# First half's projected attention tiles: scale and shift on ScalarE with a shift from Pool

## The chip, the cores and the metric

The kernel runs on one core of a Trainium2 chip. The core has five engines that each work through a queue of their own, in order: TensorE (PE, matrix products; PEld is its loading of weights), VectorE (DVE), ScalarE (ACT), GpSimd (POOL) and SyncE (SP, which here issues DMAs). An instruction that waits for a semaphore holds up all that stands behind it in its queue. The metric is the device time in microseconds (us) of one execution; the median of several runs is taken. TensorE adds up its products in PSUM, eight banks of 128 x 512 fp32 numbers.

## The reference

One transformer block on x of 8 x 1024 x 512 in fp32, causal attention with 16 heads of 32, and a feed-forward part with a sine in it:

```python
x = x + _layernorm(_L0_attn_ref(_layernorm(x), Wqvk, Wo))
x = x + _layernorm(_L0_ffn_ref(_layernorm(x), W1, b1, phases, w_real, w_imag, W2, b2))
# _layernorm: (x - mean) / sqrt(var + 1e-5), over the last axis
# _L0_attn_ref: qvk = h @ Wqvk; scores = q k^T, causal mask, / sqrt(512); softmax; @ v; @ Wo
# _L0_ffn_ref: hidden = x @ W1 + b1; hidden + coef * sin(theta + 0.1 hidden); relu; @ W2 + b2
```

The change lies in the first line, in the outer `_layernorm`: the attention's output, projected by Wo, is normalised row by row and then added to x.

## The kernel before, in words

The batches are worked one after the other (the loop at the end of `tile_block_kernel`, L923). For a batch, `attention` runs over four groups of four heads. In a group, `find_maxima` forms the row maxima of the scores, and then the scores are computed a second time, transposed, in units of keys: three units for the first half of the 512 + 512 queries, seven for the second half (`KEY_UNITS`, L428; the sixth holds key blocks 5 and 7). `weigh` does one unit: a product with minus one subtracts the maximum (L577), a second adds the scores (L588), both into two PSUM tiles of two banks; ScalarE takes the exponential of each PSUM tile into `w` (L603), and for key blocks on the diagonal Pool blanks the upper triangle (L607). `weighted_values` multiplies with v (L626), one unit later than the scores. In the second half the softmax's denominators are formed by adding up the `w` tiles on VectorE (L655), and one product with ones at the end (L641).

`finish_block` projects a half of the queries by Wo and does both layer norms around it, four tiles of 128 rows each, as a generator of stages. Stage by stage, one tile apart, these are: `project` (four products, L771; ScalarE copies the result to `ys`, L780; VectorE forms mean and variance, `moments`, L225 and L226; the reciprocal root), `add` (normalise y, L785 by way of `normalised` at L244, and add to x, L786), moments of the new x, `scale` (normalise x into `xn`, L244) and `transpose` (on TensorE, L111, with a copy by ScalarE, L262, into `x2T`, the feed-forward part's input). In each step of the generator the later stages come first.

For the first half of the queries, half 0, the generator is advanced inside the last head group, once per unit of keys of the second query half, from its second unit on. So this chain on VectorE and ScalarE runs interleaved with the exponentials L603, the selections L607 and the adds L655. Half 1 is worked in the beginning of the feed-forward part. The reciprocal root is formed by ScalarE in half 0, as exp(-0.5 ln(var + eps)) (`rstd_by_scalar`, L239 and L240), and by Pool in half 1 (`rstd_of`, L232 and L233).

The feed-forward part (`feed_forward`) runs over 2 x 16 chunks: products with W1 (L819), Identity with the bias on ScalarE (L827), the reduction of the angle on VectorE, the sine on ScalarE (L834, with its own table load once per batch), the combination on VectorE (L837, L838), and products with W2 (L846).

Two things set the order of the work. `in_order` pins an instruction to its place among the pinned ones of its engine; what is not pinned is placed by the scheduler of the tile framework by its own costs, as are the copies L780, the moments and the roots. And PSUM banks are handed out by `psum` to the tile that is free longest (L81): the second PSUM tile of a unit's scores uses the banks that the first exponential of the unit before it empties. The tiles `yp`, `xn`, `inverse` and `xin` share a pool of five buffers.

Of the kernel before, what the change touches and what calls it, by code (L numbers as in the profile page):

```python
# [11 lines left out]
F32 = mybir.dt.float32  # L12
BF16 = mybir.dt.bfloat16
AF = mybir.ActivationFunctionType
ALU = mybir.AluOpType

P = 128
# [14 lines left out]
def kernel(  # L32
# [14 lines left out]
    nc = tc.nc  # L47
# [22 lines left out]
    small = ctx.enter_context(tc.tile_pool(name="small", bufs=4))  # L70
# [10 lines left out]
    def psum(shape, dtype=F32):  # L81
        size = math.prod(shape[1:]) * (2 if dtype == BF16 else 4)
        n = -(-size // (4 * HALF))
        free = [k for k in range(0, 8, n) if None not in done_at[k : k + n]]

        def rank(k):
            halved = n == 1 and done_at[k ^ 1] is None and done_at[k] + 2 <= clock[0]
            return not halved, max(done_at[k : k + n])

        k = min(free, key=rank)  # L90
        t = banks[:, k : k + n, :].rearrange("p b n -> p (b n)")[:, : size // 4]
        if dtype != F32:
            t = t.bitcast(dtype)
        if len(shape) == 3:
            t = t.rearrange("p (a b) -> p a b", a=shape[1])
        done_at[k : k + n] = [None] * n
        banks_of[id(t)] = list(range(k, k + n)), t
        return t

    def drained(t, n=None):  # L100

        mine = banks_of[id(t)][0]
        for k in [mine[0]] if n is None and len(mine) == 1 else mine if n is None else [mine[n]]:
            clock[0] += 1
            done_at[k] = clock[0]

    def in_order(instruction):
        tc.keep_in_program_order(instruction)
# [56 lines left out]
    for n in range(2):  # L165
        t = const.tile([P, TPB, P], BF16, tag=f"parts_q{n}", name=f"parts_q{n}")
# [55 lines left out]
    def moments(src, mv):  # L222

        st = small.tile([P, 6], F32, tag="st", name="st", bufs=3)
        nc.vector.bn_stats(st, src)  # L225
        nc.vector.bn_aggr(mv, st)  # L226
# [16 lines left out]
    def normalised(dst, src, mv, rs):  # L243
        return nc.vector.tensor_scalar(dst, src, mv[:, 0, 0:1], rs, ALU.subtract, ALU.mult)  # L244

    def one_mv():
        return small.tile([P, 1, 2], F32, tag="mv1", name="mv1", bufs=6)

    def staged(n, *stages):


        for s in range(n + len(stages) - 1):
            for k in reversed(range(len(stages))):
                if 0 <= s - k < n:
                    stages[k](s - k)
            yield True

    def transpose_rows(src, dst, evacuate):
        pt = psum([P, KC, P])
        for kc in range(KC):  # L260
            transpose_on_pe(pt[:, kc, :], src[:, kc * P : (kc + 1) * P], ident)
        evacuate(dst, pt)  # L262
        drained(pt)
# [489 lines left out]
    def finish_block(b, half, wvT, x2T):  # L753


        x2T[half] = tp.tile([P, KC, HALF], F32, tag="t", name=f"x2T_{b}_{half}")
        ys, xns, mvs, rss = {}, {}, {}, {}

        def x(t):
            return xt[b, half * TPB + t]  # L760

        def measure(t, source):
            mvs[t] = one_mv()
            moments(source, mvs[t][:, 0, :])
            rss[t] = (rstd_of if half else rstd_by_scalar)(mvs[t], 1)

        def project(t):
            y = psum([P, D])
            for kc in range(KC):
                in_order(  # L770
                    nc.tensor.matmul(  # L771
                        y,
                        wvT[:, kc, t * P : (t + 1) * P],
                        wo_sb[:, kc, :],
                        start=(kc == 0),
                        stop=(kc == KC - 1),
                    )
                )
            ys[t] = tmp.tile([P, D], F32, tag="tmp", name="yp")
            nc.scalar.copy(ys[t], y)  # L780
            drained(y)
            measure(t, ys[t])

        def add(t):
            in_order(normalised(ys[t], ys[t], mvs[t], rss[t]))  # L785
            in_order(nc.vector.tensor_add(x(t), x(t), ys[t]))  # L786

        def scale(t):
            xns[t] = tmp.tile([P, D], F32, tag="tmp", name="xn")
            normalised(xns[t], x(t), mvs[t], rss[t])  # L790

        def transpose(t):
            transpose_rows(xns[t], x2T[half][:, :, t * P : (t + 1) * P], nc.scalar.copy)

        return staged(TPB, project, add, lambda t: measure(t, x(t)), scale, transpose)


# [125 lines left out]
    for b in range(B):  # L923
        load_tables()
        wvT = [tp.tile([P, KC, HALF], F32, tag="t", name=f"wvT_{b}_{n}") for n in range(2)]
        x2T = {}

        def after(g, b=b, wvT=wvT, x2T=x2T, rest=rest):


            if g == 0:
                return rest, len(KEY_UNITS[0])
            if (b, g) == (0, 1) and B > 1:
                return measure_ahead(1), 2
            if g == NG - 2 and b + 1 < B:
                return norm1(b + 1), 0
            if g == NG - 1:
                return finish_block(b, 0, wvT[0], x2T), len(KEY_UNITS[0]) + 1
            return iter(()), 0

        before = attention(b, wvT, after)
        rest = feed_forward(b, x2T, before, finish_block(b, 1, wvT[1], x2T))
# [44 lines left out]
```

## Time and profile before

| what | value |
|---|---|
| median of 3 runs | 3884.76 us (3884.75 to 3884.77) |
| the profiled execution's own time | 3884.87 us |
| its span in the trace | 3883.2 us |
| TensorE (PE) busy | 98% |
| VectorE (DVE) busy | 71% |
| ScalarE (ACT) busy | 40% |
| Pool busy | 15% |
| TensorE clock granted | 0.996 of full speed |
| DVE normalising `yp` (L244) | 64 instructions, 540 ns each |
| one batch, from one first L771 to the next | 479.0 us (259.27 to 738.31) |

A group's line in the profile has the source line, the engine, the operation, what it writes and reads, the shapes and the count, then the busy time in us and the mean of one in ns, then how long the engine stood idle just before them and what ended that. A line of the waits names who waited for whom, the time in total, the number of times and the longest. A line of a timeline has start and duration in us, the instruction and, in brackets, the idle time before it. The line numbers are those of the kernel before; helpers such as `normalised` (L244), `moments` (L225, L226) and `transpose_on_pe` (L111) serve several callers, so the tile's name tells which.

### The profile page before, as it was taken

What the parts mean: (1) busy time and instruction counts of PE and PEld (TensorE: products, weight loads), DVE (VectorE), ACT (ScalarE), POOL (GpSimd) and SP (SyncE); (2) the same over time, 40 slices, a digit from 0 to 9 for tenths busy, and PEclk for the clock granted to TensorE, in tenths of its full rate; (3) what the DMA queues carried; (4) which work ended last, traced back from release to release, by engine and by line L of the source; (5) the groups of instructions that cost most, each with busy time, mean ns of one, the idle gap of its engine ahead of it and who ended that gap; (6) DMA issues with size and microseconds to landing.
All of it is one profiled execution on the core that took longest, in us unless ns stands there. A gap on an engine that the chain in (4) does not pass through costs nothing. (4 is left out here: it accounts for less than half of the span.)

```text
span 3883.2 us, 51435 instructions
## 1 busy us (share of the span) xinstructions
PE 3800.5 (98%) x19457; PEld 1764.2 (45%) x19457; DVE 2748.0 (71%) x6105; ACT 1542.1 (40%) x2960; POOL 567.7 (15%) x1060
## 2 busy tenths in 40 slices
PE   8999999999999999999999999999999999999998
PEld 4444444444444444444444444444444444454443
DVE  4777767777676777767777677777677776777666
ACT  4552145521465214642156421564215642156311
POOL 1211021110211102111022100211002120021100
PEclk9999999999999999999999999999999999999999
DMA  4000000000000001000010000100001000000000
GB/s 155 26 20 22 22 31 11 16 22 22 31 15 12 22 22 33 12 12 22 22 33 12 12 22 22 34 12 12 22 22 33 12 12 0 22 23 12 1 0 22
DMA packets 43495, 86.42 MB, mean 22 GB/s; under 512 B 4144, under 2 KB 4208, under 8 KB 42736
## 3 DMA queue, kind: packets, MB, share of 16 engines
q1 hardware_dynamic: 39056, 71.61, 5.8%
q10 hardware_dynamic: 4192, 11.53, 0.8%
q8 instruction: 152, 2.49, 0.3%
q14 instruction: 95, 0.78, 0.1%
HBM read 66.36 MB, written 16.78 MB: 21 GB/s over the span
## 5 line engine op out<-in xcount | busy, mean ns | idle before, releaser
L819 PE MATMUL banks<-x2T,w_sb 128*128 128x512 f32 x2048 | 921.6, 593 | 5.8 <-ACT x2T L262 5.8
L846 PE MATMUL banks<-w_sb,hid 128*128 128x512 f32 x1536 | 690.5, 592 | 0.0
L603 ACT ACTIVATE w<-banks 128x1024 f32<-128x1024 f32 (+1 forms) x640 | 565.7, 937 | 241.7 <-PE banks L588 236.9
L819 PEld LDWEIGHTS banks<-x2T,w_sb 128*128 128x128 f32 x2048 | 386.0, 190 | 478.4 <-issue 468.8
L655 DVE TENSOR_TENSOR w<-w 128x1024 f32<-128x1024 f32 (+2 forms) x448 | 443.9, 1028 | 212.1 <-PE banks L626 125.3
L502 DVE CUSTOM_DVE_ANT_0 es<-banks,mask 128x128 f32<-128x128 f32 (+3 forms) x1024 | 433.0, 486 | 125.5 <-PE banks L472 125.5
L834 ACT ACTIVATE u<-u 128x512 f32<-128x512 f32 x256 | 161.1, 629 | 865.3 <-DVE u L196 842.1
L373 PE MATMUL banks<-xnT,wqvk_sb 128*128 128x512 f32 x1024 | 480.9, 609 | 3.0 <-DVE mx L490 3.0
L846 PEld LDWEIGHTS banks<-w_sb,hid 128*128 128x128 f32 x1536 | 291.8, 190 | 367.4 <-issue 328.4
L607 POOL TENSOR_SCALAR_AFFINE_SELECT w<-w 128x256 f32<-128x256 f32 x512 | 285.2, 576 | 881.6 <-ACT w L603 835.3
L490 DVE TENSOR_REDUCE mx<-banks 128x1 f32<-128x512 f32 (+1 forms) x384 | 309.9, 862 | 103.8 <-PE banks L472 103.8
L827 ACT ACTIVATE hid<-banks,prm 128x512 f32<-128x512 f32 x256 | 175.5, 686 | 473.6 <-PE banks L819 473.5
L829 DVE TENSOR_SCALAR u<-hid,prm 128x512 f32<-128x512 f32 x256 | 123.9, 484 | 308.0 <-ACT hid L827 308.0
L626 PE MATMUL banks<-w,v 128*32 128x512 f32 (+3 forms) x3072 | 325.5, 499 | 5.2 <-POOL w L607 4.3
L588 PE MATMUL banks<-qk 32*128 32x512 f32 (+3 forms) x3072 | 327.7, 491 | 0.0
L472 PE MATMUL banks<-qk 32*128 32x512 f32 (+3 forms) x3072 | 315.2, 510 | 0.6 <-DVE mx L502 0.6
L837 DVE SCALAR_TENSOR_TENSOR hid<-u,coef,hid 128x512 f32<-128x512 f32 x256 | 192.0, 750 | 161.7 <-ACT u L834 161.7
L373 PEld LDWEIGHTS banks<-xnT,wqvk_sb 128*128 128x128 f32 x1024 | 182.8, 190 | 243.3 <-issue 186.7
L522 ACT ACTIVATE es<-es,mx 128x512 f32<-128x512 f32 (+3 forms) x512 | 279.6, 551 | 2.0 <-DVE mx L502 2.0
L394 PEld LDWEIGHTS banks<-wqvk_sb,xnT 128*128 128x128 f32 x2048 | 239.0, 192 | 57.9 <-issue 34.4
L394 PE MATMUL banks<-wqvk_sb,xnT 128*128 128x128 f32 x2048 | 259.5, 280 | 0.0
L771 PE MATMUL banks<-wo_sb,wvT 128*128 128x512 f32 x512 | 234.3, 600 | 0.0
(102 smaller groups left out, 3408.3 us busy)
## 6 DMA issues: line engine op xcount, KB each, us to landing
xin<-in_L_attn_h_dram SPq DMA_DIRECT2D x112, 256.0 KB, 2.8
x<-in_L_attn_h_dram SPq DMA_DIRECT2D x64, 256.0 KB, 2.6
out_dram<-x SPq DMA_DIRECT2D x64, 256.0 KB, 2.0
w_tail<-in_L_ffn_W_dram SPq DMA_DIRECT2D x8, 1024.0 KB, 5.3
w_sb<-in_L_ffn_W_dram ACTq DMA_DIRECT2D x1, 4096.0 KB, 15.5
wqvk_sb<-in_L_attn_Wqvk_dram ACTq DMA_DIRECT2D x3, 1024.0 KB, 9.5
w_sb<-in_L_ffn_W_dram ACTq DMA_DIRECT2D x1, 3072.0 KB, 25.3
wo_sb<-in_L_attn_Wo_dram ACTq DMA_DIRECT2D x1, 1024.0 KB, 6.1
```

The source lines that it names most:

```text
L373: nc.tensor.matmul(pq, wqvk_sb[:, kc, c0 : c0 + P], xnT[b, half][:, kc, :], start=(kc == 0), stop=(kc == KC - 1),)
L394: nc.tensor.matmul(pv[:, t - t0, :], xnT[b, t // TPB][:, kc, (t % TPB) * P : (t % TPB + 1) * P], wqvk_sb[:, kc, c0 : c0 + P], start=(kc == 0),
L472: nc.tensor.matmul(scs[j // 2][:, j % 2, at : at + n], t[r, 0, i * P : (i + 1) * P], t[r, 1, k0 : k0 + n], start=True, stop=True,)
L490: nc.vector.tensor_reduce(out=mx[:, m], in_=sc[:, m, cols], op=ALU.min, axis=mybir.AxisListType.X,)
L502: nc.vector.tensor_tensor_reduce(out=es[:, m, cols], in0=sc[:, m, cols], in1=mask[:, HALF - n :], scale=1.0, scalar=FMAX, op0=ALU.add, op1 ...
L588: nc.tensor.matmul(sts[j // 2][:, j % 2, cols], t[r, 1, kb * P : (kb + 1) * P], t[r, 0, q0 : q0 + n], start=False, stop=True,)
L603: in_order(nc.scalar.activation(w[:, :, :width], st[:, :, :width], AF.Exp, scale=-1.0))
L607: select = nc.gpsimd.affine_select(out=square, in_=square, compare_op=ALU.is_ge, fill=0.0, base=0, pattern=[[0, 2], [1, P]], channel_multi ...
L626: nc.tensor.matmul(acc[r, HALF - n :], v[b, g][:, kb, r], weights[j // 2][:, j % 2, cols], start=first and k == 0, stop=last and k == len( ...
L655: in_order(nc.vector.tensor_add(t[:, :, q], t[:, :, q], w[:, :, cols]))
L819: nc.tensor.matmul(ph, w1_sb[:, kc, fc * P : (fc + 1) * P], x2T[half][:, kc, :], start=(kc == 0), stop=(kc == KC - 1),)
L846: nc.tensor.matmul(ys[half, t], hids[c // 2][:, c % 2, t * P : (t + 1) * P], w2_sb[:, fc, :] if fc < NW2 else w2_tail[:, fc - NW2, :], sta ...
```

## The change

For half 0, the four tiles of each batch that are worked inside the last head group, y is no longer normalised by one VectorE instruction with two operations, (y - mean) x rstd. Instead Pool forms a column of shifts, mean x rstd x (-1), behind the moments and the root of each tile, and ScalarE writes y x rstd + shift over y, as an Identity with a scale and a bias per partition. The addition to x stays on VectorE. Both new instructions are pinned to the program order. Half 1 is as before.

```diff
-        ys, xns, mvs, rss = {}, {}, {}, {}
+        ys, xns, mvs, rss, shifts = {}, {}, {}, {}, {}
...
             measure(t, ys[t])
+            if half == 0:
+
+                shifts[t] = small.tile([P, 1], F32, tag="rs1", name="shift", bufs=4)
+                in_order(
+                    nc.gpsimd.tensor_scalar(
+                        shifts[t], mvs[t][:, 0, 0:1], rss[t][:, 0:1], -1.0, ALU.mult, ALU.mult
+                    )
+                )
 
         def add(t):
-            in_order(normalised(ys[t], ys[t], mvs[t], rss[t]))
+            if half == 0:
+                in_order(
+                    nc.scalar.activation(
+                        ys[t], ys[t], AF.Identity, bias=shifts[t], scale=rss[t][:, 0:1]
+                    )
+                )
+            else:
+                in_order(normalised(ys[t], ys[t], mvs[t], rss[t]))
             in_order(nc.vector.tensor_add(x(t), x(t), ys[t]))
```

The shifts take their buffers from the pool `small`, under the tag of the single roots `rs` (four buffers of 128 x 1 that the roots and the shifts now share).

## The prediction

> **What bounds the kernel now.** I read the engine shares first, then the list of waits for TensorE, then the timeline of one batch around the change on each engine, then the groups by form for the prices.
>
> ```profile
> span 3883.2 us, 51435 instructions
> PE 3800.5 (98%) x19457; PEld 1764.2 (45%) x19457; DVE 2748.0 (71%) x6105; ACT 1542.1 (40%) x2960; POOL 567.7 (15%) x1060
> ...
> PE banks L577 <- ACT w L603: 20.1, 34, 1.7
> ```
>
> TensorE (PE) is busy 98% of the span. A change on the other engines is worth only what it does to PE's gaps, and the largest gap that recurs is the wait of L577 for L603: 20.1 us. The timelines of single batches show where it lies: in each of the eight batches one wait of 1.74 or 1.75 us, in the last attention group, which is where the change works. In batch 0 (start, duration, work; the bracket is the idle time before it):
>
> ```profile
> 280.34 0.34 PE L577 MATMUL banks<-mT,minus 32*128 32x384 bf16 x4
> ...
> 285.20 0.39 PE L577 MATMUL banks<-mT,minus 32*128 32x256 bf16 x2 [1.75 <-ACT w L603]
> ```
> ```profile
> 280.44 0.59 ACT L780 COPY yp<-banks 128x512 f32<-128x512 f32 x1 [1.08 <-PE banks L771]
> 283.52 0.48 ACT L239 ACTIVATE rs<-mv,eps 128x1 f32<-128x1 f32 x2 [2.49 <-DVE mv L226]
> 283.91 0.33 ACT L240 ACTIVATE rs<-rs 128x1 f32<-128x1 f32 x2
> 284.15 1.92 ACT L603 ACTIVATE w<-banks 128x1024 f32<-128x1024 f32 x2
> ```
> ```profile
> 277.43 0.55 DVE L244 TENSOR_SCALAR yp<-yp,mv,rs 128x512 f32<-128x512 f32 x1 [0.51 <-ACT rs L240]
> 278.01 0.69 DVE L786 TENSOR_TENSOR x<-x,yp 128x512 f32<-128x512 f32 x1
> 279.01 1.23 DVE L655 TENSOR_TENSOR w<-w 128x1024 f32<-128x1024 f32 x1 [0.30 <-POOL w L607]
> 280.53 1.23 DVE L655 TENSOR_TENSOR w<-w 128x1024 f32<-128x1024 f32 x1 [0.30 <-POOL w L607]
> 281.68 0.54 DVE L244 TENSOR_SCALAR xn<-x,mv,rs 128x512 f32<-128x512 f32 x1
> ```
>
> I call the key units of the second query half U0 to U6, and the four tiles 0 to 3. PE can't write the second half of U6's scores until the first exponential of U5 (L603) has emptied its banks. U5's scores are there at about 281.6, but ScalarE (ACT) reaches that exponential only at 284.15: ahead of it in its queue stands the logarithm of tile 3's variance (L239), which waits 2.49 us for VectorE's (DVE) moments. So the chain is DVE's queue, then ACT's queue, then PE. PE has no slack in it: whatever delays ACT ahead of U5's exponential delays PE, one for one.
>
> **What the change removes.** 4 x 8 = 32 normalisations on DVE, 540 ns each by the group L244 yp: 17.3 us of DVE, of which at most the three ahead of tile 3's moments (3 x 0.54 = 1.6 us a batch) lie on the chain.
>
> **What it adds.** 32 ACT instructions and 32 shifts of 128x1 on Pool. The nearest rows:
>
> ```profile
> L827 ACT ACTIVATE hid<-banks,prm 128x512 f32<-128x512 f32 x256 | 175.5, 686 | 473.6 <-PE banks L819 473.5
> ...
> L662 ACT ACTIVATE inverse<-inverse 128x512 f32<-128x512 f32 x32 | 20.2, 630 | 1.0
> L660 ACT ACTIVATE inverse<-banks 128x512 f32<-128x512 f32 x32 | 19.1, 597 | 72.7 <-PE banks L641 72.7
> ```
> ```profile
> L232 POOL TENSOR_SCALAR rs<-mv x136: 215/226/1962, 4.9 to 3876.9; 128x1 f32<-128x1 f32 x136
> ```
>
> L827 is the same function with one per-partition operand, from PSUM; L660 has none: 686 - 597 = 89 ns for an operand. From SBUF, as here, without one: 630 (L662). With bias and scale both per partition: 630 + 2 x 89 = 0.81 us. [...] Priced by L827 as it stands it would be 0.69, and the sum below 0.12 x 8 = 1 us smaller; I take 0.81. No table load: Identity already runs in this kernel beside Sin without one of its own, and the instruction order of the built program has no more loads than before. A shift costs 0.23 us (median of L232), up to 1.96 at the worst. Roots and shifts now share four buffers, so every fifth one waits for the readers of the first; the tightest, tile 3's shift in the buffer of tile 2's root, comes at 285.2 in the walk below, 5 us after its last reader: no cost. No DMA is added or moved past another; one load of the input (L306) per batch gains a wait for ACT on its buffer, for an instruction that ended long before. PE's order is identical.
>
> **What it moves.** The instruction order on ACT now reads, for tile t: copy, logarithm and exponential for tile t, logarithm for x of tile t-1, first exponential of the scores, exponential for x, Identity, second exponential of the scores. For tile 3 the Identity stands ahead of both exponentials of U5. On DVE the add x + y now waits for ACT, and for tiles 1 and 2 it stands between the two L655 adds. I walk batch 0 from the rows above (hand-over of 0.03 to 0.1 us as the rows show; back-to-back ACT work overlaps by 0.09).
>
> Tile 0: Identity at 266.9, right after U2's exponentials, done 267.7; DVE is in L655 until 268.4. Hidden: the next step on DVE waits for the copy at 269.4 anyway.
>
> Tile 1: logarithm at 270.83 (before 270.90). U3's first exponential ends 272.46. DVE has been empty since 270.94; before, it filled that gap with the normalisation and the add. Now L655, add, L655 and xn start at 272.50; from start to start they take 1.14 + 0.60 + 1.14 + 0.46, so the next moments begin at 275.84, not 275.43: 0.41 late. That is what DVE gives back: 0.55 less work, but it begins 1 us later.
>
> Tile 2: logarithm at 277.23, U4's first exponential 277.86 to 278.86, Identity to 279.68, second exponential to 280.59 (before 279.36). Pool's first selection ends 279.37; DVE L655 to 280.63, add to 281.24. Pool's second selection comes in only behind DVE's two-input work, about 0.26 us after it (as at 279.48 to 280.50 before): 281.5. The second L655 starts 281.53, before 280.53: DVE is now 1.0 us late, and tile 3's moments are ready at 284.51.
>
> Tile 3: logarithm 284.53, exponential to 285.06, logarithm and exponential for x of tile 2 to 285.50; the shift meanwhile, 285.16 to 285.40, while DVE waits; Identity 285.41 to 286.22; U5's first exponential starts at 286.13. Before: 284.15. **Late by 1.98 us**, of which 1.01 is DVE's lag and 0.97 the longer chain on ACT. PE's wait grows from 1.75 to about 3.7 us.
>
> Behind it: Pool's selections of U5, of which five of the eight batches lost 0.24 + 0.41 us before (L626 waits for L607). Now the second exponential comes when DVE is in L655, so one selection can hold PE for up to 0.5 us, while U6's exponentials come early and the 0.65 goes. 8 x 0.5 - 5 x 0.65 = 0.8 us at one end, -3.3 at the other; I take zero. The sums at L641 need the adds, done at about 292.3, and PE comes there at about 293.2: covered by 0.9 us. In the feed-forward part PE has dense work and the chain starts anew.
>
> Sum: 8 x 1.98 = 15.8 us on the profiled execution's 3884.87 us (1.7 us more than its span; the median of the runs is 3884.76): 3900.7, say **3901**. With 0.6 of DVE lag and 0.69 of Identity it is 1.45 a batch, 3896.5; with a shift held up by one DVE instruction (0.54) and the 0.5 for the selection 3.0 a batch, 3909. Own range 3896 to 3910.
>
> **The rivals.**
> Relief of DVE (not slower). If DVE were the queue that counts and always had work, tile 3's moments would come 1.62 us earlier, at 281.9; with the same ACT chain of 1.60 us U5's exponential starts at 283.5, 0.65 earlier than now: 8 x 0.65 = 5.2, 3880. If Identity also hid, the whole 1.75 would go: 8 x 1.75 = 14, 3871. [...] The trace's windows give DVE 27.6 us busy of 45.3 from 255.34 to 300.66, 61%: busy, not saturated, and its stops are for ACT. It decides where U3's and U4's first exponentials come before DVE runs empty: for U3 some 1.5 us earlier than I find (DVE empty at 270.94, exponential done at 272.46). 12%, half of it faster by over 0.2%.
> Only the chain. DVE makes up its lag, and 0.97 a batch remains: 8 x 0.97 = 7.8, 3893. For it: my 0.6 us at the second selection rests on a Pool operation that yields. 10%.
> Pool is starved. L232's longest of 1.96 us and L607's 1.02 beside L655 against 0.41 alone show that Pool waits for DVE:
>
> ```profile
> 278.57 0.41 POOL L607 TENSOR_SCALAR_AFFINE_SELECT w<-w 128x256 f32<-128x256 f32 x1 [25.39 <-ACT w L603]
> 279.48 1.02 POOL L607 TENSOR_SCALAR_AFFINE_SELECT w<-w 128x256 f32<-128x256 f32 x1 [0.51 <-ACT w L603]
> ```
>
> A shift of tile 3 of 1.96 instead of 0.23 adds 1.7 us, tile 2's some 0.2: 3.9 a batch, 8 x 3.9 = 31, 3916. It decides once tile 3's shift ends later than 285.41. Against it: at all four moments DVE stands idle waiting for ACT (264.6, 271.4, 277.8, 285.2). 10%.
>
> **How the numbers follow.** 68% for 3901, 12% for relief, 10% for only the chain, 10% for starvation. A measurement of this kernel tells about 0.2% (7.8 us) from no change. Faster 6%; same 11% (the other half of relief, half of only the chain); slower 83%. The range from 3886 to 3918 leaves out relief and the upper end of starvation, some 15%.
>
> **What would show it.** L577's wait for L603 goes from 20.1 to about 36 us, one wait of about 3.7 us a batch; DVE waits for ACT ahead of L655 in U3 and for Pool in U4; 32 Identities at about 0.8 us, 32 shifts at about 0.25; DVE 17 us less busy, ACT 26 us more. I am wrong if the wait in each batch shrinks, if DVE's gap ahead of U3's first L655 is not there, if the shifts last over 0.5 us, or if new waits of PE appear elsewhere.

## The result and the profile after

The changed kernel takes 3901.8 us (median of four runs, 3900.56 to 3902.84), the kernel before 3884.77 us (four runs, 3884.75 to 3885.04): a ratio of 1.0044, 95% interval 1.0031 to 1.0056. It is slower by 17 us. The profiled execution of after took 3900.56 us, 15.7 us more than that of before.

The page of after, in the rows that answer to those of before:

```profile
PE 3803.5 (98%) x19457; PEld 1766.5 (45%) x19457; DVE 2735.3 (70%) x6073; ACT 1565.9 (40%) x2992; POOL 572.8 (15%) x1092
...
PE banks L577 <- ACT w L603: 36.3, 34, 3.8
```

VectorE is 12.7 us less busy (17.3 us of normalisations gone, other instructions some 4.6 us longer in sum), ScalarE 23.8 us more. PE's instructions are the same, and its wait at L577 for L603 has grown from 20.1 to 36.3 us. That is 16.2 us, about as much as the whole loss; how much of it each batch really pays is taken up below. The timelines of batch 0 show where it comes from. TensorE first (the whole trace of this batch starts 0.56 us earlier than before: the first L771 is at 258.71, it was at 259.27):

```profile
279.78 0.34 PE L577 MATMUL banks<-mT,minus 32*128 32x384 bf16 x4
...
286.69 0.40 PE L577 MATMUL banks<-mT,minus 32*128 32x256 bf16 x2 [3.79 <-ACT w L603]
```

The wait of 1.75 us has become 3.79 us; it is 3.79 or 3.80 in each of the eight batches. ScalarE in the same stretch:

```profile
279.89 0.58 ACT L780 COPY yp<-banks 128x512 f32<-128x512 f32 x1
283.93 0.29 ACT L239 ACTIVATE rs<-mv,eps 128x1 f32<-128x1 f32 x1 [3.45 <-DVE mv L226]
...
284.91 0.81 ACT L795 ACTIVATE yp<-yp,shift,rs 128x512 f32<-128x512 f32 x1
285.63 1.92 ACT L603 ACTIVATE w<-banks 128x1024 f32<-128x1024 f32 x2
```

Two things are to be seen. The logarithm of tile 3 starts at 283.93; with the 0.56 us added it is 284.49, against 283.52 before: 0.97 us late, because VectorE's moments are late. And between that logarithm and U5's first exponential there now lie 1.70 us (283.93 to 285.63), where there were 0.63: 1.07 us more, and with the 0.97 that is the 2.04 us of the wait. Why the moments are late stands in VectorE's timeline:

```profile
271.94 1.22 DVE L655 TENSOR_TENSOR w<-w 128x1024 f32<-128x1024 f32 x1 [1.56 <-ACT w L603]
...
278.81 1.23 DVE L655 TENSOR_TENSOR w<-w 128x1024 f32<-128x1024 f32 x1 [2.04 <-POOL w L607]
279.95 0.68 DVE L801 TENSOR_TENSOR x<-x,yp 128x512 f32<-128x512 f32 x1
280.93 1.23 DVE L655 TENSOR_TENSOR w<-w 128x1024 f32<-128x1024 f32 x1 [0.30 <-POOL w L607]
```

VectorE has nothing to do for 1.56 us ahead of U3's first addition and for 2.04 us ahead of U4's, and the addition x + y stands between the two additions of U4, with Pool's second selection behind it. The time that VectorE no longer spends on normalising has turned into waiting.

**What the batch pays.** I call the time from a batch's first L771 to half 1's first L771, which stands behind the sums L641, the group's time. The sums need VectorE's last addition L655. These lines are from batch 0, first in before and then in after (PEld is TensorE's loading of weights):

```profile
289.40 1.82 DVE L655 TENSOR_TENSOR w<-w 128x256 f32<-128x256 f32 x3
...
291.28 0.14 PEld L641 LDWEIGHTS banks<-w,ones 128*32 128x32 f32 x4 [0.19 <-DVE w L655]
292.26 3.70 PE L771 MATMUL banks<-wo_sb,wvT 128*128 128x512 f32 x8
```
```profile
290.36 1.82 DVE L655 TENSOR_TENSOR w<-w 128x256 f32<-128x256 f32 x3
...
293.22 3.70 PE L771 MATMUL banks<-wo_sb,wvT 128*128 128x512 f32 x8
```

In before, TensorE comes to the sums 0.28 us ahead of that addition's end and waits for it, and half 1 begins 1.04 us after it: the addition ends 31.95 us into the group, and the group's time is 32.99 us, in all eight batches. The same 1.04 us are found in every batch of six of the kernels below, and less in no batch of any. So it is VectorE's last addition that bounds the group in before, and not the wait at L577 alone. VectorE works up to it from tile 3's normalisation on (284.13 to 291.22) with no stop over 0.10 us, so the addition does not wait for TensorE. In after it ends 33.47 us into the group, which is 1.52 us later and not 2.04. Of this, 0.97 are the late moments, and 0.55 lie behind them, where VectorE now waits for the root of x and then for Identity (from tile 3's logarithm to the end of the last addition it is 7.70 us before and 8.25 after). In batch 0 half 1 begins 1.04 us behind the addition, as before, at 34.51 us; in the other batches it begins later, up to 35.56. The mean is 35.01 us, 2.02 more than before, or 16.2 us over eight batches; less the 0.56 us by which batch 0 starts earlier, these are the 15.7 of the profiled executions. So 1.52 us a batch come by way of VectorE, and 0.50 in the mean from something else, which the experiment on the clock shows below. That the sum is as large as the growth of the wait is chance.

The prices of the new instructions, from the list of the tile `shift`:

```profile
L787 POOL TENSOR_SCALAR shift<-mv,rs x32: 264/264/266, 264.6 to 3640.5; 128x1 f32<-128x1 f32 x32
L795 ACT ACTIVATE yp<-yp,shift,rs x32: 801/808/815, 266.3 to 3640.8; 128x512 f32<-128x512 f32 x32
```

A correction to the description of the kernel above, as far as the orders in these traces show it: `in_order` pins an instruction behind the one that the program wrote just before it on the same engine, pinned or not. If that one is unpinned, it can be moved itself, and what is pinned behind it moves along. So U5's exponential is held behind tile 3's root, written one unit earlier; tile 3's Identity is written after U5's exponentials, but is held only behind an unpinned root, and the scheduler put both ahead of them.

### The profile page after: what moved, and what is told of

The parts are those of the page before. It is cut to its first block, busy times and chain, and to the rows that moved or that the text cites. A ratio compares the mean times of both kernels' runs of the same rounds, so it can differ in the third digit from the quotient of the medians.

```text
span 3898.8 us, 51417 instructions
## 1 busy us (share of the span) xinstructions
PE 3803.5 (98%) x19457; PEld 1766.5 (45%) x19457; DVE 2735.3 (70%) x6073; ACT 1565.9 (40%) x2992; POOL 572.8 (15%) x1092
## 4 chain that ended last, share of the span: by engine, by line
PE 90%; DVE 4%; ACT 3%; issue 2%; POOL 1%; DMA 0%; POOLq 0%; SPq 0%; ACTq 0%
PE banks L834 23%; PE banks L861 22%; PE banks L373 12%; PE banks L472 7%; PE banks L394 6%; PE banks L626 5%; PE banks L588 5%; PE banks L771 4%; PE banks L577 2%; ACT w L603 2%; DVE mx L490 2%; PE banks L111 2%; DVE st L225 1%; PE banks L641 1%; DVE w L655 1%
## 5 line engine op out<-in xcount | busy, mean ns | idle before, releaser
L603 ACT ACTIVATE w<-banks 128x1024 f32<-128x1024 f32 (+1 forms) x640 | 567.1, 937 | 242.2 <-PE banks L588 237.3
L655 DVE TENSOR_TENSOR w<-w 128x1024 f32<-128x1024 f32 (+2 forms) x448 | 446.5, 1032 | 237.7 <-PE banks L626 125.0
L394 PEld LDWEIGHTS banks<-wqvk_sb,xnT 128*128 128x128 f32 x2048 | 239.1, 192 | 57.8 <-issue 34.3
L771 PE MATMUL banks<-wo_sb,wvT 128*128 128x512 f32 x512 | 234.3, 600 | 0.0
```

The lines of the kernel that those rows point to most:

```text
L394: nc.tensor.matmul(pv[:, t - t0, :], xnT[b, t // TPB][:, kc, (t % TPB) * P : (t % TPB + 1) * P], wqvk_sb[:, kc, c0 : c0 + P], start=(kc == 0),
L603: in_order(nc.scalar.activation(w[:, :, :width], st[:, :, :width], AF.Exp, scale=-1.0))
L655: in_order(nc.vector.tensor_add(t[:, :, q], t[:, :, q], w[:, :, cols]))
L771: nc.tensor.matmul(y, wvT[:, kc, t * P : (t + 1) * P], wo_sb[:, kc, :], start=(kc == 0), stop=(kc == KC - 1),)
```

## The experiments

Each was run with the kernel before on the same chip; "before" has 3884.67 to 3884.94 us in all of them. Line numbers in the lines shown are those of the kernel in question.

**One part of the change alone: tile 3, or tiles 0 to 2.** In the changed kernel both places are restricted:

```diff
-            if half == 0:
+            if half == 0 and t == 3:      # the other kernel: t < 3
```

> Only tile 3 of each batch goes by Pool and ScalarE, tiles 0 to 2 by VectorE as before. Queue theory: VectorE is as before up to tile 3's moments (283.5 in batch 0), then ScalarE takes logarithm, exponential, logarithm, exponential, Identity before U5's exponentials: they come 0.97 us later than before, PE's wait L577 for L603 is 2.7 us a batch, the time 3884.8 + 8 x 0.97 = 3892.5. Rival, every Identity costs the same wherever it stands (the 17 us shared by 32): a quarter, 3889.1. Rival, VectorE's 0.54 us saved counts: at or below 3884.8.

> Tiles 0 to 2 of each batch go by Pool and ScalarE, tile 3 by VectorE as before. Queue theory: VectorE's lag of 1.0 us at tile 3's moments remains, the ScalarE chain behind them is that of before: PE's wait 2.75 us a batch, 3884.8 + 8 x 1.0 = 3892.8. Rival, equal cost of every Identity: three quarters of 17 us, 3897.6. Rival, relief of VectorE (1.62 us less of its work ahead of tile 3's moments): the wait all but vanishes, 3871 to 3872.

Measured: 3893.29 us (ratio 1.0021, 1.0013 to 1.0029) and 3893.88 us (1.0023, 1.0014 to 1.0032). The waits of TensorE, with tile 3 alone and then with tiles 0 to 2:

```profile
PE banks L577 <- ACT w L603: 28.2, 34, 2.8
```
```profile
PE banks L577 <- ACT w L603: 27.5, 33, 2.7
```

One batch's wait is 2.77 us with tile 3 alone, 1.02 more than before; and 2.73 with the others, 0.98 more. Together 2.00, and the full change has 2.04 more: the two delays are separate and add up, as the walk had it (0.97 and 1.01). The group's time shows what they are worth. Its least value is 33.55 us with tile 3 alone and 33.98 with the others, 0.56 and 0.99 more than before, and VectorE's last addition is later by as much. So tile 3's delay reaches the batch with little more than half its length. Some batches have a longer group's time (up to 34.54 and 34.34): in these TensorE's products behind the wait are slow for longer. Four transposes take 1.12 us in batch 1 of the first kernel (34.44 us) and 0.66 in its batch 2 (33.56); in the second kernel the four after those take 0.89 in batch 0 (34.32) and 0.66 in batch 2 (33.99). This is taken up with the clock below.

**Tile 0 alone** (`t == 0`), whose Identity the walk called hidden.

> Only tile 0 of each batch goes by Pool and ScalarE. Its Identity stands behind U2's exponentials in an idle stretch of ScalarE, and what VectorE saves it spends waiting for the next copy. Queue theory: tile 3's moments move by 0.07 us at most, 3884.2, no change that can be measured. Rival, equal cost of every Identity: 3889.

Measured: 3884.49 us (0.9999, 0.9991 to 1.0007), a wait of 1.70 us and a group's time of 32.95. The same instruction that costs 1 us a batch at tile 3 costs nothing at tile 0. A cost that is equal for every Identity is ruled out.

**Where Identity stands in ScalarE's queue.** ScalarE's roots and its copies in `finish_block` are pinned too (the copies in both halves), so that this part of its queue follows the program, which writes U5's exponentials ahead of tile 3's Identity:

```diff
-        nc.scalar.activation(rs, mv[:, :, 1], AF.Ln, bias=eps)
-        nc.scalar.activation(rs, rs, AF.Exp, scale=-0.5)
+        in_order(nc.scalar.activation(rs, mv[:, :, 1], AF.Ln, bias=eps))
+        in_order(nc.scalar.activation(rs, rs, AF.Exp, scale=-0.5))
...
-            nc.scalar.copy(ys[t], y)
+            in_order(nc.scalar.copy(ys[t], y))
```

(and likewise the copy into `x2T`), once in the changed kernel, once in the kernel before.

> The changed kernel, with the copies of y and of x2T and the logarithms and exponentials of the roots pinned too, so that ScalarE does all of this in the order in which the program writes it: both exponentials of a unit's scores together and ahead of the Identity, and U5's exponentials ahead of tile 3's Identity. Queue theory: nothing of the new work stands between tile 3's moments and U5's exponentials any more, and VectorE is late by about 0.5 us; U5's first exponential starts near 284.3 instead of 286.1 in batch 0's time of before, PE's wait is 1.9 us a batch, the time 3886. Rival, the work moved to ScalarE costs by its amount (32 x 0.81 us less 32 x 0.54 saved, or the 17 us measured): it stays at 3893 to 3902.

> The kernel before with the same pins as act_pinned, as the control for no_norm_pinned. Queue theory: the logarithm and exponential for x of tile 2 no longer stand ahead of U5's exponentials, 0.1 us a batch: 3884. Nothing else moves.

Measured: the change so pinned 3890.05 us (1.0013, 1.0007 to 1.0020), the kernel before so pinned 3881.16 us (0.9990, 0.9982 to 0.9999). With Identity behind U5's exponentials the wait is 2.16 us and not 3.79, which takes 12 of the 17 us away; but 3886 was expected, and it is 4 us above. The kernel before also gains, more than expected: its wait is 1.47 us instead of 1.75, since the root of x no longer stands ahead of U5's exponential. So against its own base the pinned change still costs 8.9 us. The group's time is 33.50 us in every batch of the one and 32.59 of the other, each 1.04 us behind VectorE's last addition: 0.91 us a batch, 7.3 of the 8.9. The moments alone are later by 0.69 (2.16 - 1.47).

**Relief of VectorE at no price.** The pinned kernel before, with the normalisation of y in half 0 left out:

```diff
-            in_order(normalised(ys[t], ys[t], mvs[t], rss[t]))
+            if half:
+                in_order(normalised(ys[t], ys[t], mvs[t], rss[t]))
```

> before_pinned without the normalisation of y in the first half, which is left out (y is added to x as it is; moments and roots are still formed): VectorE is relieved of all that the change takes from it, and ScalarE and Pool get nothing. Queue theory: VectorE waits for the exponentials of U3 and U4 anyway, so tile 3's moments come only about 0.5 us earlier: 4 us less than before_pinned, 3880. Rival, VectorE's work in front of the moments is what counts: 1.62 us earlier, the wait of 1.75 all but gone, 3871.

Measured: 3876.14 us (0.9978, 0.9970 to 0.9987), 5.0 us below the pinned kernel before, where 4 were expected. The waits of the pinned kernel before and of this one:

```profile
PE banks L577 <- ACT w L603: 17.5, 33, 1.5
```
```profile
PE banks L577 <- ACT w L603: 16.0, 34, 1.2
```

Three normalisations, 1.62 us of VectorE, are gone ahead of tile 3's moments, and TensorE's wait is 0.27 us shorter, 2.2 us over eight batches. The whole gain is in the group's time: it falls from 32.59 to 31.97 us in each batch, because VectorE's last addition, which stands behind all four normalisations, comes 0.62 us earlier, and eight times 0.62 is 5.0. So relief of VectorE is worth 0.62 of the 2.16 us a batch that are taken from it. VectorE now waits longer for ScalarE's exponentials ahead of its additions L655, 57.8 us in all instead of 51.5. By the premise of the relief rival, that VectorE's time is worth its length here, the whole wait of 1.47 us would have gone, 11.8 us; a normalisation that costs nothing on any engine brings less than half of that.

**The clock behind the longer wait.** The trace of after showed something that the walk did not have: in each of its eight batches TensorE's granted clock is half for 3.41 or 6.83 us at the end of the wait or shortly behind it. In before three batches have such a phase. Here are the parts of it behind the wait in batch 0 and in batch 6 of after (start and end, length, then busy time and count of PE, PEld, DVE, ACT, POOL, the granted clock, the DMA share, GB/s):

```profile
286.69:290.08 3.39, 3.39 (x24) 1.36 (x25) 3.25 (x6) 2.59 (x6) 3.23 (x5) 0.50 0.20 46
```
```profile
3172.38:3177.76 5.38, 5.38 (x38) 2.27 (x37) 5.24 (x9) 3.06 (x7) 3.86 (x6) 0.50 0.56 171
```

To see what this is worth, the products of U6's first two heads, which do not need the missing banks, were written five times over, so that TensorE works through a part of its wait:

```diff
-            for j in range(HPG):
+            first = g == NG - 1 and keys == (6,)
+            for js in (5 * [(0, 1)] + [(2, 3)]) if first else [range(HPG)]:
+                for j in js:
...
```

> The changed kernel; in the last head group U6's first two heads have both their products ahead of the other two heads', and these are done five times over (the same result each time), so that TensorE works through most of its wait of 3.8 us. If the wait lets TensorE's clock fall, the granted clock behind it is near 1.00 instead of 0.50, L588 takes 0.71 again instead of 1.24, and with 0.36 us of real work now done within the wait the time falls by 8 x 0.36 + 6 x 0.5 = 6 us to 3896. If the clock has another cause: 3899, with the clock at 0.50 as before.

Measured: 3900.37 us (1.0040, 1.0027 to 1.0052), above both expectations, 1.4 us below after and within its scatter. The wait is 1.18 us now, and right behind it the clock is full. But it was not kept: in seven of the eight batches it falls to half 0.7 to 2.0 us later. Batch 4 of this kernel, from the end of the wait on:

```profile
2210.75:2212.66 1.91, 1.48 (x10) 0.46 (x9) 1.77 (x4) 1.91 (x5) 1.75 (x4) 1.00 0.22 8
2212.67:2216.08 3.41, 3.41 (x24) 1.48 (x24) 3.41 (x6) 1.08 (x3) 2.10 (x3) 0.50 0.81 303
```

So the run does not show what a full clock would be worth, except in batch 7, which has no such phase: its group's time is 34.51 us, as in batch 0 of after, where the phase is over early. In the other batches of after the time follows the end of the phase, and in the kernel with the repeated products nearly the same ends give the same times within 0.03 us:

| batch of after | 0 | 1 | 2 | 3 | 4 | 5 | 6 | 7 |
|---|---|---|---|---|---|---|---|---|
| half clock ends, us behind the wait | 3.40 | 4.10 | 4.70 | 5.01 | 5.22 | 5.33 | 5.38 | 6.23 |
| group's time, us | 34.51 | 34.63 | 34.92 | 35.02 | 35.11 | 35.17 | 35.19 | 35.56 |

TensorE's transposes of the next tile in batch 0, where the clock is full again, and in batch 6, where it is not yet:

```profile
290.30 0.66 PE L111 MATMUL banks<-ident,xn 128*128 128x128 f32 x4
```
```profile
3176.14 1.12 PE L111 MATMUL banks<-ident,xn 128*128 128x128 f32 x4
```

VectorE's last addition is at 33.47 or 33.48 us in all of them. A half clock that ends early is hidden behind it; one that lasts makes TensorE come later than VectorE. Over 34.51 us the eight batches have 4.0 us in sum, and this is the 0.50 us a batch that was left open above. In before, all eight batches take 32.99 us, three of them with such a phase (it ends at 4.49 us behind the wait at the latest, where VectorE's last addition ends at 6.02): there it costs nothing. What lowers the clock is not shown. It fell near waits of 3.79, 1.75 and 1.18 us, and in batch 1 of the kernel with late roots below it did not near one of 1.92.

**Taking the root out of U5's way.** The kernel before, with ScalarE's queue pinned as above, and y's root written in `add`, one unit later than the moments:

```diff
-            rss[t] = (rstd_of if half else rstd_by_scalar)(mvs[t], 1)
+            if half or source is not ys[t]:
+                root(t)
...
         def add(t):
+            if half == 0:
+                root(t)
```

> The kernel before, VectorE normalising, with the logarithm and exponential of y's root written one stage later (in add instead of project) and ScalarE's work in these stages pinned to the order in which it is written: U5's exponentials then come ahead of tile 3's logarithm. Queue theory: PE's wait of 1.75 us in each batch goes, 8 x 1.75 = 14 us, 3871. If tile 3's moments only reach PE another way (the sums L641 waiting for VectorE's adds, the transposes waiting for xn), 3878 to 3885.

Measured: 3876.80 us (0.9979, 0.9970 to 0.9987). TensorE's waits at L577, and its timeline at the end of batch 1:

```profile
PE banks L577 <- ACT w L603: 6.3, 26, 0.6
```
```profile
766.67 0.66 PE L111 MATMUL banks<-ident,xn 128*128 128x128 f32 x4 [1.92 <-DVE xn L244]
```

The wait of 1.75 us that every batch of before has at L577 is gone: it came from the place of tile 3's root, and no engine was made faster. A new wait of 1.92 us has come for it, for tile 2's `xn`, which VectorE now reaches late. The gain is 8 us all the same, and not the 14 of the whole wait: the group's time is 31.76 us in every batch instead of 32.99 (9.8 us over eight batches in the profiled execution, which took 3874.33). The old wait was not worth its length, since VectorE's last addition stood behind it.

**The change on that base**: the root, Pool's shift and Identity together in `add`.

```diff
         def add(t):
             if half == 0:
                 root(t)
-            in_order(normalised(ys[t], ys[t], mvs[t], rss[t]))
+                shifts[t] = small.tile([P, 1], F32, tag="rs1", name="shift", bufs=4)
+                in_order(nc.gpsimd.tensor_scalar(shifts[t], mvs[t][:, 0, 0:1], rss[t][:, 0:1], -1.0, ALU.mult, ALU.mult))
+                in_order(nc.scalar.activation(ys[t], ys[t], AF.Identity, bias=shifts[t], scale=rss[t][:, 0:1]))
+            else:
+                in_order(normalised(ys[t], ys[t], mvs[t], rss[t]))
```

> The changed kernel with y's root, the shift and the Identity all written one stage later (in add) and ScalarE's work in these stages pinned to the order in which it is written: U5's exponentials come ahead of tile 3's logarithm and Identity, and on VectorE the xn of tile 2 no longer stands behind a normalisation of tile 3. Queue theory: the 1.75 us go, and most of the 1.92 us that the transposes waited for xn in late_roots_pinned; the Identity of tile 3 now stands ahead of U6's exponentials and holds PE there by up to 0.7 us: 3867 (3862 to 3872), faster than late_roots_pinned with the same change that cost 17 us elsewhere. Rival, work on ScalarE in this stage costs by its amount: slower than late_roots_pinned, 3880 or more.

Measured: 3877.87 us (0.9982, 0.9975 to 0.9990). The gain expected of it did not come. The list of the tile `shift`, then ScalarE and TensorE in batch 1:

```profile
L793 POOL TENSOR_SCALAR shift<-mv,rs x32: 612/1023/1322, 266.7 to 3620.0; 128x1 f32<-128x1 f32 x32
```
```profile
758.15 0.81 ACT L798 ACTIVATE yp<-yp,shift,rs 128x512 f32<-128x512 f32 x1 [1.60 <-POOL shift L793]
```
```profile
766.04 0.62 PE L626 MATMUL banks<-w,v 128*32 128x256 f32 x4 [1.68 <-POOL w L607]
```

Here the rival that Pool is starved has come true, in another kernel: the shift is asked for while VectorE is in its additions L655, takes 0.61 to 1.32 us where it took 0.26, and holds ScalarE (39.2 us of waiting over the 32 shifts). At the end U6's exponentials, the selections and TensorE are late.

**The same without Pool**: ScalarE forms the shift itself, in two instructions of 128x1.

```diff
-                    nc.gpsimd.tensor_scalar(
-                        shifts[t], mvs[t][:, 0, 0:1], rss[t][:, 0:1], -1.0, ALU.mult, ALU.mult
+                    nc.scalar.activation(
+                        shifts[t], mvs[t][:, 0, 0:1], AF.Copy, scale=rss[t][:, 0:1]
...
+                in_order(nc.scalar.activation(shifts[t], shifts[t], AF.Copy, scale=-1.0))
```

> late_roots_act with the shift formed by two 128x1 instructions on ScalarE (mean times root, then times -1) instead of one on Pool. If Pool's shift held the Identity there because it waits behind VectorE's two-input work (0.61 to 1.32 us instead of 0.26, and ScalarE idle 0.8 to 1.6 us for it), U6's exponentials come some 0.7 us earlier and PE's wait of 1.68 us for its selection shrinks to about 0.8: 8 x 0.8 = 6 us less than late_roots_act, 3872. If the Identity's 0.81 us itself is what is late: no change, 3878.

Measured: 3869.23 us (0.9960, 0.9946 to 0.9973), the fastest of all, 15.7 us below the kernel before in the same comparison, and 32.6 us below the changed kernel. ScalarE in batch 1:

```profile
761.66 0.30 ACT L793 ACTIVATE shift<-mv,rs 128x1 f32<-128x1 f32 x1
761.99 0.20 ACT L797 ACTIVATE shift<-shift 128x1 f32<-128x1 f32 x1
762.22 0.81 ACT L799 ACTIVATE yp<-yp,shift,rs 128x512 f32<-128x512 f32 x1
762.94 1.06 ACT L603 ACTIVATE w<-banks 128x512 f32<-128x512 f32 x2
```

About 0.6 us of ScalarE takes the place of a shift of up to 1.3 us. Tile 3's shift and Identity, shown here, are out of the way of U5's exponentials, but still stand ahead of U6's, and TensorE has one wait of 1.37 us for Pool's selection of U6 left. The group's time is 31.12 us, 1.04 behind VectorE's last addition.

**The other way to remove the 1.92 us**: the late roots on VectorE, with x's normalisation written one stage earlier.

```diff
+        def measure_and_scale(t):
+            measure(t, x(t))
+            scale(t)
+
+        if half == 0:
+            return staged(TPB, project, add, measure_and_scale, lambda t: None, transpose)
```

> late_roots_pinned (VectorE normalises y, as before the change) with the normalisation of x written one stage earlier, right behind the moments of x, so that tile 2's xn stands ahead of tile 3's normalisation on VectorE. Queue theory: PE's wait of 1.92 us for xn goes; the sums L641 then wait about 1.0 us for the last adds on VectorE: 8 x 0.9 = 7 us less than late_roots_pinned's 3876.8, 3870.

Measured: 3872.32 us (0.9967, 0.9954 to 0.9979). The 1.92 us are gone in all eight batches, and a wait of 0.85 at L641 for VectorE's last addition is there instead. That confirms what held TensorE in the kernel with late roots; both ways together were not tried.

## Why the prediction was right, point by point

- **What bounds the kernel.** The delay was walked rightly: L577's wait for L603 is 2.04 us longer in each batch, 1.98 predicted. That TensorE has no slack in it and pays it one for one is not so. Behind it VectorE's last addition bounds the group, in before already, and where the clock is full again in time the batch grows by 1.52 us and not by 2.04. The half clock, which the walk did not have, adds 0.50 in the mean. The total of 2.02 us a batch agrees with the 1.98 predicted by luck.
- **VectorE's lag, 1.01 us a batch.** Right: 0.97 in the trace, 0.98 in the wait and 0.99 in the group's time with tiles 0 to 2 alone. The idle time ahead of U3's first addition was predicted (1.56 us) and so was the place of tile 2's addition between the two of U4.
- **ScalarE's longer chain, 0.97 us a batch.** Right as a delay: 1.07 in the trace of after, 1.02 with tile 3 alone; U5's exponential came at 286.19 on before's scale, 286.13 predicted. As a cost it is too large: the batch pays 0.55 or 0.56 of it.
- **Prices.** Identity 0.81 us (808 ns measured), as built up from L827, L660 and L662. Priced by L827 as it stands it would have been 0.69. The shift 0.264 us, and never held up, because VectorE stands idle when it is asked for. ScalarE's busy time rose by 24 us, not 26, VectorE's fell by 13, not 17.
- **Relief of VectorE.** Falls: the kernel is slower. Taking the work away altogether moves the wait by 0.27 us and the batch by 0.62, of 2.16 taken away. What is true in it is that VectorE's additions bound the group's end.
- **Only the chain.** Falls as a description of the whole: VectorE does not make up its lag. It describes tile 3's part of the wait.
- **Pool is starved.** Falls in this kernel, for the reason given against it. Its mechanism is there in another kernel: asked for during L655, the shift took 0.61 to 1.32 us instead of 0.264.
- **Behind the wait, taken as zero.** Near zero, but by two terms that cancel. From the wait's end to half 1 it took 7.06 us before, and in after 6.53 where the clock is full in time: 8 x 0.53 = 4.2 us less, more than the 3.3 at the lower end of the prediction. The half clock gives 4.0 us back. The walk had the sums L641 covered by 0.9 us. They are not: on before's scale TensorE comes there at 292.60 and the last addition ends at 292.74, and in before it is the same (290.94 and 291.22).

## What to carry to other kernels

Before work is moved to an idle engine, read what stands behind it in that engine's queue and who waits for that: here the same Identity cost nothing at one tile, 1 us of TensorE's wait at another, and was part of the fastest kernel once it was queued behind the exponentials that TensorE waited for. Here an engine that is 71% busy but stops for others gave little when it was relieved, 0.62 of 2.16 us a batch; walk one period of the schedule and see whether its freed time becomes a wait. The longest wait need not be what bounds the stretch: look for what comes at a fixed distance ahead of its end in every batch, here a last addition that the profile names with a wait of 0.19 us. And look for the cause of the wait itself: here it was the place of one small root in a queue, and moving that gained 8 us with no change of who does the arithmetic.

## What the runs showed of the hardware

- A 128x1 operation on Pool, the shift, took 0.264 us with VectorE idle (after, L787), and 0.61 to 1.32 us when asked for during VectorE's two-input additions L655 (the change on late roots, L793).
- TensorE's granted clock was half at the wait or within 2.1 us behind it in all eight batches of after (wait 3.79 us), in three of before (1.75 us) and in seven of the kernel with repeated products (1.18 us), for 3.413 or 6.827 us at a time. The starts of these phases in after lie whole multiples of 3.413 us apart (286.67 and 767.95, for one, by 141 of them), while its first six batches are 480.57 to 481.23 us long, so the phase falls elsewhere in each batch. No such phase stands behind the wait of 1.92 us in batch 1 of the kernel with late roots, where the four transposes took 0.66 us and the next eight products (L641) 1.06. What lowers the clock is not shown.
- Four transposes took 0.66 us at the full clock and 1.12 at half. Half the clock cost a batch nothing where VectorE's last addition came later still (32.99 us in all batches of before), and up to 1.05 us where it outlasted that (34.51 to 35.56 us in after).
